# Turning the softmax maxima: a PE transpose in the first gap, or a float32r product in the gap of the first values

## Chip, cores and metric

The kernel is one program for one core of a Trainium2 chip. The metric is device time in microseconds (us) of one execution on that core, taken as the median of several runs. The engines that matter here are PE (TensorE, the matrix engine; the profile lists its weight loads apart, as PEld), ACT (ScalarE), DVE (VectorE), POOL (GpSimd) and SP, which here only issues DMAs.

## What is computed

The reference is one transformer block on 32 sequences of 512 tokens and 256 channels. Attention has 16 heads of 16 channels and two passes; the second pass attends over the error that the first one leaves. A small mixture of experts follows, which only touches the first sequence, and two layer norms. Cut to what matters here:

```python
qk = x @ W_attn + b_attn                      # q and k, 16 heads of 16
y  = softmax(mask(q @ k.T / sqrt(16))) @ v    # v = x by heads
e  = v[1:] - y[:-1]
k2 = x[:-1] @ W_k2 + b_k2
y2 = softmax(mask(q[1:] @ k2.T / sqrt(16))) @ e
x  = layernorm(x + proj(y) + proj(y2))
x  = layernorm(x + experts(x))                # experts: first sequence only
```

A softmax over keys needs the largest score of each query row. In the kernel these largest scores are the "maxima".

## The kernel before

**Groups and steps.** Four heads of one sequence are a group, so there are 32 x 4 = 128 groups. The function `step(n)` runs 132 times and works on several groups at once, as a pipeline: it finds the maxima of group n, computes the exponentials of group n-1 (first pass) and n-2 (second pass), and multiplies the exponentials of group n-2 with the values.

**Slots and gaps.** A step has five slots. A slot (`slot(n, s)`) is a stretch of small PE products that use 32 rows of the array each: score products for the maxima, which go to the PSUM tiles `sm` (L297, and their causal masks, L282), and score products for the exponentials, which go to the PSUM tiles `sc` (L361). The four heads are handled as two pairs. `slot` writes the order of these products out by hand: pair 1's exponentials and pair 0's maxima come first, then pair 0's exponentials and pair 1's maxima. Behind the maxima's products DVE finds the largest score of each row (L321, into `top`); behind the exponentials' products ACT takes the exponential (L378, `sc` to `pt`), four instructions in a slot.

After each slot comes a gap: products that use the whole array. The list `rest[s]` holds what is called in gap s. Gap 0 holds `augment(n-1)` in every step. In odd steps, half of a projection follows it (`project`, tile `pj`, L219, read out by ACT at L231 into `pk`). In even steps it is a quarter of an output projection (`attended`, tile `po`, L522, read out by DVE at L525 into `h`). Gap 1 holds the first values, `values(n-2, 0)` (tile `av`, L430), gaps 2 and 3 hold transposes of the attended values (`yt`, L445) and more of the projections, and gap 4 the second values. Eight steps, from n = 12 on, hold a part of one expert in front of this (`gu`, L603, and others).

**The maxima's way.** DVE splits each maximum into two halves that float32r holds exactly, a rounded one and the rest (`halve`, L327 and L328, called at the end of gap 4), in the tile `mx`. `augment` in the next step turns `mx` with four 128x128 PE transposes into one PSUM bank, the tile `mt` (L334), and ACT copies it to SBUF as `m` (L336). The score products take `m` as a third term, `k == 2`, with a matrix of minus ones as the stationary operand, so that what comes out is score minus maximum. The products of slots 0 and 1 use the `m` of group n-2. Slot 2 is the first one that uses the `m` of group n-1: its third product of each stream.

**PSUM.** There are eight banks. Four of them are two pairs for `sm` (`pair_of_banks`, two buffers). The other four (`bank`, four buffers) are taken in rotation by everything else, in the order in which the products are written: four `sc` tiles in each slot, and one for each full-array tile in a gap. A product may write to its bank only after the tile that had it before has been read out.

```python
def bank(name):
    return psum.tile([P, T], F32, tag="one", name=name, bufs=4)
```

**Who sets the order.** PE's and SP's order is the order of the code (`manual_schedule`). On ACT, DVE and POOL a planner sets the order. A tile framework puts in all waits. `half(ap)` is a view of float32 data as float32r.

Of the kernel before, what the change touches and what calls it, by code (L numbers as in the profile page):

```python
# [9 lines left out]
F32 = mybir.dt.float32  # L10
# [7 lines left out]
P = 128  # L18
# [16 lines left out]
def half(ap):  # L35
    return ap.bitcast(F32R)
# [3 lines left out]
def block_kernel(  # L40
# [16 lines left out]
    nc = tc.nc  # L57
# [10 lines left out]
    const = ctx.enter_context(tc.tile_pool(name="const", bufs=1))  # L68
# [10 lines left out]
    def bank(name):  # L79
        return psum.tile([P, T], F32, tag="one", name=name, bufs=4)  # L80
# [60 lines left out]

    ident = const.tile([P, P], F32, name="ident")
    make_identity(nc, ident)
    mhalf = const.tile([P, NB], F32, name="mhalf")
    nc.gpsimd.memset(mhalf, -0.5)

# [31 lines left out]
    mx = [const.tile([P, NB, GH, HS], F32, name=f"mx{i}") for i in range(2)]  # L178
# [12 lines left out]
    def load(b):  # L191
        if b:
            load_turned(b)
        s = seqs[b]
        s["x"] = seq.tile([P, NB, C], F32, tag="x", name=f"x{b}")
        nc.sync.dma_start(s["x"], x[b].rearrange("(n p) c -> p n c", p=P))

    def load_next(b):

        s = seqs[b]  # L200
        s["xs"] = seq.tile([P, NB, C], F32, tag="xs", name=f"xs{b}")
        nc.sync.dma_start(s["xs"][:, 0 : NB - 1], x[b, 1 : T - P + 1].rearrange("(n p) c -> p n c", p=P))
        nc.sync.dma_start(s["xs"][0 : P - 1, NB - 1], x[b, T - P + 1 : T])
        nc.sync.dma_start(s["xs"][P - 1 : P, NB - 1], x[b, T - 1 : T])

    def prepare(n):
        b, g = divmod(n, NG)
        s = seqs[b]
        heads = slice(g * GH, (g + 1) * GH)
        nc.gpsimd.tensor_copy(  # L210
            by_head(v_pad)[:, :, heads, 0:HD], s["x"].rearrange("p n (h d) -> p n h d", d=HD)[:, :, heads]
        )
# [26 lines left out]
    def spread(two, m, which=range(2)):  # L239

        for k in which:
            n = 2 * two + k
            d = groups.setdefault(n, {})
            d["q"] = q_t[n % len(q_t)]
            d["kk"] = kk_t[n % len(kk_t)]
            rows = slice(k * GH * HD, (k + 1) * GH * HD)
            for i, t in enumerate(moving[two, m]):
                if m == 0:
                    for r in range(2):
                        nc.sync.dma_start(d["q"][r::2, i], t[rows])  # L250
                else:
                    nc.sync.dma_start(d["kk"][i::2, m - 1], t[rows])
        if 1 in which:
            del moving[two, m]
# [70 lines left out]
    def halve(n):  # L325
        t, top = mx[n % 2], groups[n]["top"]
        nc.vector.tensor_copy(half(t[:, :, :, 0:2]), top)  # L327
        nc.vector.tensor_sub(half(t[:, :, :, 2:4]), top, t[:, :, :, 0:2])  # L328

    def augment(n):  # L330
        d = groups[n]
        ps = bank(f"mt{n}")
        for i in range(NB):
            nc.tensor.transpose(ps[:, i * P : (i + 1) * P], mx[n % 2][:, i].rearrange("p h s -> p (h s)"), ident)  # L334
        d["m"] = grp.tile([P, T], F32, tag="m", name=f"m{n}")
        nc.scalar.copy(half(d["m"]), ps)  # L336

# [102 lines left out]
    def normalize(n, a):  # L440
        b, g = divmod(n, NG)
        d, s = groups[n], seqs[b]
        ps = bank(f"yt{n}_{a}")
        for i in range(NB):
            nc.tensor.transpose(ps[:, i * P : (i + 1) * P], d["avs", a][:, i * P : (i + 1) * P], ident)  # L445
        got = ps.rearrange("p (n h s) -> p n h s", h=GH, s=HS)
        if a:

            kept = work.tile([P, NB, GH, HV], F32, tag="kept", name=f"kept{n}", bufs=2)
            nc.scalar.copy(kept, got[:, :, :, 0:HV])  # L450
            got = kept
        rden = small.tile([P, NB, GH], F32, tag="rden", name=f"rden{n}_{a}")
        sums = got[:, :, :, HD]
        if a:

            den = small.tile([P, NB, GH], F32, tag="den", name=f"den{n}")
            nc.vector.tensor_scalar_max(den, sums, 1e-30)
            sums = den
        nc.vector.reciprocal(rden, sums)
        rb = rden.unsqueeze(3).to_broadcast([P, NB, GH, HD])  # L460
        cols = slice(g * GH * HD, (g + 1) * GH * HD)

        def heads(t):
            return t[:, :, cols].rearrange("p n (h d) -> p n h d", d=HD)

        if a == 0:
            if g == 0:
                s["y"] = seq.tile([P, NB, C], F32, tag="y", name=f"y{b}")
            nc.vector.tensor_mul(heads(s["y"]), got[:, :, :, 0:HD], rb)
            nc.gpsimd.tensor_sub(by_head(e_pad)[:, :, g * GH : (g + 1) * GH, 0:HD], heads(s["xs"]), heads(s["y"]))  # L470
        else:
            y2 = work.tile([P, NB, GH * HD], F32, tag="y2", name=f"y2_{n}", bufs=1)
            nc.vector.tensor_mul(y2.rearrange("p n (h d) -> p n h d", d=HD), got[:, :, :, 0:HD], rb)
            nc.gpsimd.tensor_add(s["y"][:, :, cols], s["y"][:, :, cols], y2)  # L474
            groups.pop(n)
# [174 lines left out]
    def step(n):  # L650
        ready = lambda k: 0 <= k < n_all
        rest = [[] for _ in units]
        b, r = divmod(n, NG)
        if r == 1 and b + 1 < B:
            load(b + 1)
        if r == 3 and b + 1 < B:
            load_next(b + 1)
        if ready(n):
            prepare(n)
        if ready(n - 3):  # L660
            rest[3].append(lambda: normalize(n - 3, 1))
        if ready(n):
            rest[4].append(lambda: halve(n))
        if ready(n - 1):
            rest[0].append(lambda: augment(n - 1))
        if ready(n - 2):
            soon = n > n_all
            rest[0 if soon else 1].append(lambda: values(n - 2, 0))
            rest[1 if soon else 2].append(lambda: normalize(n - 2, 0))
            rest[4].append(lambda: values(n - 2, 1))  # L670
        two = n // 2 + 1
        if ready(2 * two):
            if n % 2 == 0:
                rest[2].append(lambda: project(two, 1))
                rest[4].append(lambda: spread(two, 1))
            else:
                rest[2] += [lambda: project(two, 0), lambda: spread(two, 0)]
                rest[0].append(lambda: project(two, 2, 0, T // 2))
                rest[3] += [lambda: project(two, 2, T // 2), lambda: spread(two, 2)]
        b, r = divmod(n - 3, NG)  # L680
        if r == NG - 1 and 0 <= b < B:
            rest[4].append(lambda b=b: turn(b))

        for b in range(B):
            end = (b + 1) * NG - 1
            last = b == B - 1
            for part in range(2):
                if n == (end + 4 if last else min(end + 5 + 2 * part, n_all)):
                    for i in range(2 * part, 2 * part + 2):
                        rest[0 if last or i % 2 == 0 else 3].append(lambda b=b, i=i: attended(b, i))  # L690
                if n == (end + 3 if last else end + 4):
                    rest[1 + 2 * part].append(lambda b=b, part=part: biased(b, part))
            if n == (end + 2 if last else end + 3):
                rest[3].append(lambda b=b: load_residual(b))
            if 0 < b < B - 1 and n == end + 8:
                rest[1].append(lambda b=b: store(b))


        e = n - first_expert
        if e == -1:  # L700
            rest[4] += [route, turn_tokens, lambda: load_hidden(0), lambda: load_down(0)]
        if e == 0:
            rest[0].insert(0, biases)
        if 0 <= e < E:
            rest[3].insert(0, lambda: hidden(e, 0, 0))
            rest[4].insert(0, lambda: hidden(e, 0, 1))
        if 0 <= e - 1 < E:
            rest[0].insert(0, lambda: hidden(e - 1, 1, 0))
            rest[1].insert(0, lambda: hidden(e - 1, 1, 1))
            rest[2].insert(0, lambda: down(e - 1))  # L710
            if e < E:
                rest[1].append(lambda: load_hidden(e))
                rest[2].append(lambda: load_down(e))
        if e == E:
            rest[4].append(lambda: second_norm(0, moe["acc"]))
        for s in range(len(units)):
            slot(n, s)
            for f in rest[s]:
                f()
# [94 lines left out]
```

## Time and profile before

| what | value |
|---|---|
| median of 3 runs | 2659.15 us (2658.19 to 2659.2) |
| the profiled execution | 2655.88 us |
| its span, first to last instruction | 2654.2 us |
| mean granted TensorE clock | 0.990 of full speed |
| POOL busy | 1730.8 us, 65% of the span |
| transposes of the maxima, L334 | 512, in 128 sets of four |
| copies to `m`, L336 | 128, 78.7 us of ACT in all |

A line of the timeline has a start (us from the start of the trace), a length (us, from the first start to the last end of what is merged), engine, line, operation, the tile written and the tiles read, shapes and a count; in brackets the engine's idle time before it and what ended that. The matmuls' ends are modelled, and matmuls overlap, so on PE the starts tell more than the lengths. In a weight load or matmul such as `mt<-ident,mx` the moving operand stands first and the stationary one second. The chain of work follows the last instruction back through what released each step.

### The profile page before, as it was taken

To read this page: it belongs to the slowest core of one execution; us is meant where nothing else is said; L and a number is where in the kernel's file an instruction comes from. 1 tells how busy PE (TensorE), PEld (TensorE's weight loads), DVE (VectorE), ACT (ScalarE), POOL (GpSimd) and SP (SyncE) were. 2 spreads that over 40 slices of the span, in tenths; PEclk is the share of its full clock that TensorE was granted. 3 is DMA by queue.
4 is the path that set the end of the run, shared out by engine and by line. 5 is a ranking of instruction groups with operands and counts; after the bars stand their busy time and mean duration, and the time that the engine had idled before them with its cause. 6 is when DMAs were issued, how large, how long until landed. Compare 5 with 4: busy or idle time off the path is not lost.

```text
span 2654.2 us, 98011 instructions
## 1 busy us (share of the span) xinstructions
PE 2593.7 (98%) x41488; PEld 1800.0 (68%) x41488; DVE 1936.3 (73%) x3225; ACT 1757.9 (66%) x3416; POOL 1730.8 (65%) x3303
## 2 busy tenths in 40 slices
PE   7999999999999999999999999999999999999997
PEld 4666666667676666666677667666776767677765
DVE  6767777677777777777777777777777777777773
ACT  3766544467667766766776677676777667677774
POOL 4555555466666667666666666666766666676664
PEclk8999999999999999999999999999999999999998
DMA  5323233233333333333333333342333334333320
GB/s 142 88 75 85 73 89 95 70 85 102 81 92 87 93 94 82 102 84 83 96 86 101 82 97 89 75 105 82 99 88 93 93 75 104 82 90 96 88 67 25
DMA packets 167461, 233.26 MB, mean 88 GB/s; under 512 B 21528, under 2 KB 91152, under 8 KB 167024
## 3 DMA queue, kind: packets, MB, share of 16 engines
q1 hardware_dynamic: 164592, 226.54, 32.9%
q8 instruction: 329, 5.39, 0.9%
q14 instruction: 108, 0.88, 0.1%
q10 hardware_dynamic: 2368, 0.42, 0.1%
q0 software_dynamic: 64, 0.02, 0.0%
HBM read 75.41 MB, written 16.78 MB: 35 GB/s over the span
## 4 chain that ended last, share of the span: by engine, by line
PE 90%; ACT 5%; issue 2%; DVE 2%; POOL 1%; DMA 0%; ACTq 0%; POOLq 0%; SPq 0%; DVEq 0%
PE av L430 22%; PE sc L361 20%; PE pj L219 13%; PE sm L297 10%; PE sm L282 7%; PE yt L445 6%; ACT pt L378 5%; PE po L522 4%; PE mt L334 3%; PE gu L603 2%; PE ys L511 1%; PE dn L626 1%; DVE top L321 1%; POOL xr L503 0%; POOL h L544 0%
## 5 line engine op out<-in xcount | busy, mean ns | idle before, releaser
L321 DVE TENSOR_REDUCE top<-sm 128x2 f32<-128x768 f32 (+3 forms) x1800 | 1536.4, 907 | 611.2 <-PE sm L297 610.6
L378 ACT ACTIVATE pt<-sc 128x512 f32<-128x512 f32 (+1 forms) x2564 | 1323.8, 601 | 333.8 <-PE sc L361 198.0
L382 POOL TENSOR_SCALAR_AFFINE_SELECT pt<-pt 128x256 f32<-128x256 f32 x2048 | 789.9, 410 | 520.2 <-ACT pt L378 519.8
L297 PE MATMUL sm<-kk_t,q_t 32*128 32x512 f32 (+2 forms) x7168 | 1100.0, 382 | 16.7 <-DVE top L321 9.3
L361 PE MATMUL sc<-q_t,kk_t 32*128 32x256 f32 (+3 forms) x8192 | 1028.2, 334 | 3.0 <-DVE h L525 1.8
L361 PEld LDWEIGHTS sc<-q_t,kk_t 32*128 32x128 f32 x8192 | 678.5, 184 | 257.5 <-issue 160.2
L361 PE MATMUL sc<-m,minus 32*128 32x256 f32 (+3 forms) x4096 | 694.6, 318 | 0.0
L297 PEld LDWEIGHTS sm<-kk_t,q_t 32*128 32x128 f32 x7168 | 567.6, 185 | 23.1 <-DVE top L321 12.2
L282 PE MATMUL sm<-hide,pick 32*128 32x64 bf16 (+5 forms) x10240 | 517.7, 217 | 0.0
L361 PEld LDWEIGHTS sc<-m,minus 32*128 32x128 f32 x4096 | 441.2, 185 | 10.0
L219 PE MATMUL pj<-xT,wq_sb 128*128 128x256 f32 (+1 forms) x1020 | 397.7, 513 | 6.3 <-DVE wq_sb L112 6.3
L438 ACT COPY avs<-av 128x512 f32<-128x512 f32 x256 | 150.4, 588 | 324.7 <-PE av L430 324.7
L430 PE MATMUL av<-pt,e_pad 128*32 128x512 f32 (+3 forms) x4096 | 304.3, 437 | 7.5 <-ACT pt L378 0.8
L430 PE MATMUL av<-pt,v_pad 128*32 128x512 f32 (+3 forms) x4096 | 302.7, 435 | 8.3 <-POOL pt L382 5.0
L231 ACT ACTIVATE pk<-pj,bp_qk 128x256 f32<-128x256 f32 (+1 forms) x255 | 151.3, 593 | 190.3 <-PE pj L219 182.7
L237 POOL TENSOR_TENSOR pk<-pk,lead 128x512 fp32r<-128x512 f32 x192 | 244.9, 1276 | 14.3 <-ACT lead L236 3.6
L430 PEld LDWEIGHTS av<-pt,v_pad 128*32 128x32 f32 x4096 | 136.3, 109 | 163.0 <-issue 126.9
L282 PEld LDWEIGHTS <-pick 32*128 32x128 bf16 x10240 | 243.7, 93 | 0.9 <-issue 0.7
L219 PEld LDWEIGHTS pj<-xT,wq_sb 128*128 128x128 f32 x1020 | 175.5, 192 | 92.1 <-issue 64.3
L430 PEld LDWEIGHTS av<-pt,e_pad 128*32 128x32 f32 x4096 | 128.9, 110 | 144.0 <-issue 135.6
L474 POOL TENSOR_TENSOR y<-y,y 128x256 f32<-128x256 f32 x128 | 96.6, 755 | 125.4 <-DVE mv L538 58.0
L445 PE MATMUL yt<-ident,avs 128*128 128x128 f32 x1024 | 168.0, 287 | 6.0 <-ACT pt L378 1.0
(90 smaller groups left out, 1955.1 us busy)
## 6 DMA issues: line engine op xcount, KB each, us to landing
q_t<-lead SPq DMA_DIRECT2D x256, 128.0 KB
q_t<-pk SPq DMA_DIRECT2D x256, 128.0 KB
kk_t<-lead SPq DMA_DIRECT2D x256, 128.0 KB
kk_t<-pk SPq DMA_DIRECT2D x256, 128.0 KB
xT<-in_xT SPq DMA_DIRECT2D x32, 512.0 KB
x<-in_x SPq DMA_DIRECT2D x32, 512.0 KB
xr<-in_x SPq DMA_DIRECT2D x32, 512.0 KB
out<-h SPq DMA_DIRECT2D x31, 512.0 KB
```

Source lines behind the costliest of these rows:

```text
L219: nc.tensor.matmul(ps[:, 0 : hi - lo], wq_sb[:, m, c, part * P : (part + 1) * P], seqs[b]["xT"][:, c, lo:hi], start=(c == 0), stop=(c == N ...
L231: nc.scalar.activation(pk[:, lo:hi], ps[:, 0 : hi - lo], AF.Identity, bias=bp_qk[:, m, part : part + 1])
L237: nc.gpsimd.tensor_sub(half(pk), pk, lead)
L282: nc.tensor.matmul(ps[hh][:, 0 if alone else hh].rearrange("p (k c) -> p k c", c=P)[:, first::step, HS * c :], pick[rows, c], hide[rows, c ...
L297: nc.tensor.matmul(part(ps[hh], i, na, at)[:, 0 if alone else hh], half(d["q"][rows, k, i * P : (i + 1) * P]), half(d["kk"][rows, a : a + ...
L321: nc.vector.tensor_reduce(to, view, AX.X, ALU.max)
L361: nc.tensor.matmul(ps[hh][:, at * P : at * P + T - j * P], half(keys), half(queries[:, j * P :]), start=(k == 0), stop=(k == 2),)
L378: nc.scalar.activation(pt[:, hh, lo:hi], ps[hh][:, lo:hi], AF.Exp, scale=HD**-0.5)
L382: nc.gpsimd.affine_select(diag, diag, pattern=[[0, NH2], [1, P]], compare_op=ALU.is_ge, fill=0.0, base=-a, channel_multiplier=-1,)
L430: nc.tensor.matmul(ps[HS * h : HS * (h + 1), j * P :], vals[:, j, (g * GH + h) * HV : (g * GH + h) * HV + HS], d["pt", a, j, h // NH2][:, ...
L438: nc.scalar.copy(avs, ps)
L445: nc.tensor.transpose(ps[:, i * P : (i + 1) * P], d["avs", a][:, i * P : (i + 1) * P], ident)
```

## The change

The four transposes become four ordinary products in float32r. The stationary operand is the same block of `mx`, now read as float32r, and the moving operand is an identity that is read as float32r too; a copy of the identity is rounded for it once at the start. The call moves from `rest[0]` to `rest[1]`, where it stands in front of `values(n-2, 0)`. The ACT copy to `m` is the same and moves along.

```diff
     ident = const.tile([P, P], F32, name="ident")
     make_identity(nc, ident)
+    ident_half = const.tile([P, P], F32, name="ident_half")
+    nc.vector.tensor_copy(half(ident_half), ident)
...
     def augment(n):
         d = groups[n]
         ps = bank(f"mt{n}")
         for i in range(NB):
-            nc.tensor.transpose(ps[:, i * P : (i + 1) * P], mx[n % 2][:, i].rearrange("p h s -> p (h s)"), ident)
+            nc.tensor.matmul(
+                ps[:, i * P : (i + 1) * P],
+                half(mx[n % 2][:, i].rearrange("p h s -> p (h s)")),
+                half(ident_half),
+                start=True,
+                stop=True,
+            )
         d["m"] = grp.tile([P, T], F32, tag="m", name=f"m{n}")
         nc.scalar.copy(half(d["m"]), ps)
...
         if ready(n - 1):
-            rest[0].append(lambda: augment(n - 1))
+            rest[1].append(lambda: augment(n - 1))
         if ready(n - 2):
             soon = n > n_all
             rest[0 if soon else 1].append(lambda: values(n - 2, 0))
```

## Prediction

> **What bounds the kernel.** I read the page's busy rows and its chain first, then the waits of PE's weight loads, then the timeline of two neighbouring steps, engine by engine.
>
> ```profile
> PE 2593.7 (98%) x41488; PEld 1800.0 (68%) x41488; DVE 1936.3 (73%) x3225; ACT 1757.9 (66%) x3416; POOL 1730.8 (65%) x3303
> PE 90%; ACT 5%; issue 2%; DVE 2%; POOL 1%; DMA 0%; ACTq 0%; POOLq 0%; SPq 0%; DVEq 0%
> PEld mt L334 <- ACT pt L378: 25.5, 124, 0.5
> PEld sc L361 <- DVE h L525: 2.8, 5, 0.7
> ```
>
> PE's own work sets the time: 98% busy, 90% of the chain. DVE, ACT and POOL each idle for a quarter of the span or more, but they hand out the PSUM banks, so they can still hold PE at a certain product. Work that only moves from one gap to another should cost PE nothing; the question is which bank is not free when PE comes earlier. That needs the timeline. First an even step (output projection in gap 0): PE's rows, the load of one later product, DVE's rows and ACT's rows.
>
> ```profile
> 1320.95 0.66 PE L334 MATMUL mt<-ident,mx 128*128 128x128 f32 x4
> 1321.44 1.12 PE L522 MATMUL po<-wp_sb,ysT 128*128 128x256 f32 x4
> 1322.49 0.45 PE L361 MATMUL sc<-q_t,kk_t 32*128 32x384 f32 x2
> 1323.31 0.18 PEld L361 LDWEIGHTS sc<-q_t,kk_t 32*128 32x128 f32 x2
> 1324.40 1.07 PE L430 MATMUL av<-pt,v_pad 128*32 128x512 f32 x8
> ...
> 1320.45 2.48 DVE L321 TENSOR_REDUCE top<-sm 128x2 f32<-128x768 f32 x4 [1.08 <-PE sm L297]
> 1322.85 0.41 DVE L525 TENSOR_TENSOR h<-po,xr 128x256 f32<-128x256 f32 x1
> ...
> 1320.29 2.06 ACT L378 ACTIVATE pt<-sc 128x512 f32<-128x512 f32 x4 [0.28 <-PE sm L297]
> 1322.22 0.62 ACT L336 CAST m<-mt 128x512 fp32r<-128x512 f32 x1
> ```
>
> The turning takes PE from 1320.95 to 1321.44, 0.49 us. Slot 1 runs from 1322.49 to 1324.40, where the first values start. The load at 1323.31 is the one to watch: it is the first product of slot 1 that writes the last of its four banks, and in the rotation that bank is the one `po` had. It comes 0.05 us after the `h` addition has ended (1322.85 + 0.41 = 1323.26). So already now PE meets that addition almost to the point. The addition itself waits for no PE work any more; it stands behind slot 0's four reductions on DVE, which run without a break from 1320.45 to 1322.93.
>
> An odd step has half a projection in place of `po`; rows of ACT, DVE and the loads:
>
> ```profile
> 1303.05 0.62 ACT L336 CAST m<-mt 128x512 fp32r<-128x512 f32 x1
> 1303.51 0.52 ACT L231 ACTIVATE pk<-pj,bp_qk 128x256 f32<-128x256 f32 x1
> ...
> 1301.28 2.48 DVE L321 TENSOR_REDUCE top<-sm 128x2 f32<-128x768 f32 x4 [1.18 <-PE sm L297]
> ...
> 1303.32 0.18 PEld L361 LDWEIGHTS sc<-q_t,kk_t 32*128 32x128 f32 x2 [0.33 <-ACT pt L378]
> 1304.09 0.21 PEld L361 LDWEIGHTS sc<-q_t,kk_t 32*128 32x128 f32 x2
> 1304.17 0.20 PEld L297 LDWEIGHTS sm<-kk_t,q_t 32*128 32x128 f32 x2
> ```
>
> Here the same product (1304.09) follows the copy to `pk`, which ended at 1304.03 behind the copy to `m`.
>
> **The change, part by part.** *Out of gap 0: 0.49 us a step.* The mean wait of the first load for an exponential's bank, 25.5 us over 124 sets or 0.2 us, lies under products still in flight. `po` or `pj` takes the place and the bank of `mt`, and slot 1 could start 0.49 us earlier. Its first two banks are now those of the second and third exponential of slot 0 (before, third and fourth): the four run 0.5 us apart, the third ends near 1321.85, and slot 1 would start at 1322.00. No wait there.
>
> *Even steps: the gain meets DVE.* The last bank is still the one of `po`. Slot 0 has not moved, so the reductions still end at 1322.93 and the addition at 1323.26. Left alone, the product would load 0.77 us after the slot's start (the distance in the odd step, 1304.09 - 1303.32), at 1322.77. It must wait until 1323.31, and PE's queue is in order, so everything behind it waits too: the rest of slot 1 and gap 1. The 0.49 us are all lost, and slot 1 ends at 1324.40 as before. Then the turning, now in gap 1, comes on top.
>
> *Odd steps: the gain is kept.* ACT no longer has `m` between the exponentials and `pk`, so `pk` ends near 1303.6, and the product that needs its bank would load at 1303.32 - 0.49 + 0.77 = 1303.60: no wait worth counting. Next late is the product that loads at 1304.17, pair 1's first maxima product: it would come at 1303.68, but its `sm` banks are free only when slot 0's reductions end, 1301.28 + 2.48 = 1303.76. That is a wait of about 0.1 us, about what the present hold behind `pk` costs. The turning comes back in gap 1, so the step nets 0, within -0.05 and +0.1.
>
> *Into gap 1: 0.44 us a step.* In the steps with an expert product at the head of gap 0 the exponentials' banks come free earlier; there `mt` starts at 372.69 and `po` at 373.13 (timeline of PE). Those 0.44 us, 0.11 us for each transpose, I take as the width where nothing waits. For the new form no row exists. From below: in the groups by form `sc<-q_t,kk_t` takes 431 ns with 512 columns and 369 with 384, so 128 float32r columns stream in some 0.06 us; if only the streams counted, four would take 0.25 us. From above: loads of 183 ns (`sc<-m,minus`) that overlap with nothing, plus the streams, 0.97 us. The nearest rows are two float32r products of 128 columns, one behind the other on the same rows of the array:
>
> ```profile
> 1323.95 0.18 PEld L361 LDWEIGHTS sc<-q_t,kk_t 32*128 32x128 f32 x1
> 1324.06 0.19 PEld L361 LDWEIGHTS sc<-m,minus 32*128 32x128 f32 x1
> ```
>
> They follow each other by 0.11 us, the pitch of the transposes. These use 32 rows and the new ones 128. I take 0.44 us.
>
> A rule speaks against the swap: the Trainium skill, "Perfetto Trace Analysis", section "Transposes", says to turn data with the transpose and not with an ordinary matmul, because the transpose skips the arithmetic. "TensorE: Matmul & The Clock Gate", section "Terms", gives the mode as four times faster for FP32. Taken literally, four products would take 1.76 us and the change +1.3 us in 123 steps, +160 us more. The 0.11 us pitch of float32r above speaks against that; the rule's factor is for plain FP32. I weigh it as a rival.
>
> *What covers the rest.* In gap 1 the turning needs the bank of slot 1's first exponential and the values that of the second; the present values already take the first one, so no new wait. The copy to `m` moves behind slot 1's exponentials on ACT. In the even step they end near 1325.4 and `m` near 1326.0, while slot 2 starts no earlier than the end of the values (2.36 us long in the chain), near 1327.2: over 1 us of cover. `mx` is ready earlier still. No DMA is issued by `augment`; SP and POOL hold nothing of it and it passes nothing of theirs that waits for it. The rounded identity is one DVE copy at the start, about 0.2 us as the casts to `minus` (228 ns), while PE still waits for weights: nothing.
>
> *Sum.* `po` follows `mt` in 60 even steps and `pj` in 63 odd ones (from the code's conditions; the other 5 of the 128 count as nothing). 60 x 0.44 us = 26 us; 63 x 0 = 0. Against the profiled execution: 2655.88 (span 2654.2 and 1.7 around it) + 26 = 2682. The median of the runs lies 3.3 us above that execution, so 2685 us, +1.0%. About 0.2% (5 us) is what a measurement here can tell from no change.
>
> **Rivals.**
> *Faster, 2647 us.* If the planner put the `h` addition in front of pair 1's reductions, or the rotation gave its bank later, both kinds of step keep the earlier slot 1 and also lose the present holds. Slot 1 takes 1.91 us now (1322.49 to 1324.40), but 1.75 us in the expert step (374.09 to 375.84). With some 0.1 us saved in 123 steps: -12 us. It decides if the addition ends within 0.77 us of slot 1's start. Against it: the addition stands behind the reductions in the code as on DVE now, and their input is ready earlier.
> *No change, 2659 us.* The turning is only moved: even steps keep part of the gain, since the bank rotation or the order differs from my reading, and odd steps are neutral. For it: PE is the bound and its work is the same.
> *Far slower, 2715 us.* The loads for 128 rows don't overlap with the streams, as the rule suggests. At 0.25 us more per set (four loads at 0.183 us in place of 0.11, less the shorter last stream of 0.06 in place of 0.11), 123 sets cost 31 us on top.
> *ACT's order, 2790 us.* If the copy to `m` went behind the copy of the values (L438, 0.59 us) it would end 1.2 us after slot 2's start, while its first reader loads about 0.3 us after it: 0.85 us in 123 steps, 105 us on top. Against it: its input is ready over 2 us earlier.
>
> **Numbers.** My forecast 0.66, with 2677 to 2701 as its own range (0.35 to 0.6 us in even steps, -0.05 to +0.1 in odd ones); faster 0.12; no change 0.09; far slower 0.10; ACT's order 0.03. Slower by over 0.2% is then 0.79. For 8 in 10 I leave out the faster case and ACT's order, 0.15 together: 2656 to 2715.
>
> **What would show it.** Right: in even steps the product of slot 1 loads just behind the `h` addition, about 1.3 us after the slot's start, and the row of `sc` loads waiting for `h` grows from 2.8 us to some 30 us; in odd steps `sm` loads wait a little for `top`; the matmuls of `mt` still follow each other by 0.11 us, with loads of 183 ns in place of 140. Wrong: `h` on DVE ahead of pair 1's reductions, a pitch of `mt` near 0.2 us, or `sc` products of slot 2 that wait for `m`.

## The result, and the profile after

| | before | after |
|---|---|---|
| median | 2659.18 us (4 runs) | 2698.97 us (4 runs, 2698.35 to 2700.79) |
| span of the profiled execution | 2654.2 us | 2697.5 us |
| mean granted TensorE clock | 0.990 | 0.991 |

The ratio is 1.0164, with a 95% interval from 1.0150 to 1.0177: slower by about 40 us. The forecast was 2685 us, +26 us. The sign and the mechanism were right; the size was short by 14 us, mainly in one term, the width of the turning in its new place.

Line numbers are shifted in the changed kernel: L299 stands for the maxima's products, L221 for `pj`, L323 for the reductions, L337 for the turning, L345 for the copy to `m`, L370 for the `sc` products, L387 for the exponentials, L439 for the values, L531 for `po` and L534 for the `h` addition. In the kernels of the experiments they can be a few lines off again. First the page of the changed kernel, busy rows and chain:

```profile
PE 2629.6 (97%) x41488; PEld 1802.7 (67%) x41488; DVE 1935.5 (72%) x3226; ACT 1764.1 (65%) x3416; POOL 1730.3 (64%) x3303
PE 84%; DVE 6%; ACT 5%; issue 2%; POOL 2%; DMA 0%; ACTq 0%; POOLq 0%; DVEq 0%
```

PE's number of instructions is the same, and DVE has its one cast more. But the chain runs through DVE for 6% of the span, where it was 2%. The list of waits says at which product (waits of the weight loads, then of the matmuls):

```profile
PEld sc L370 <- DVE h L534: 23.4, 60, 0.7
...
PE sc L370 <- DVE h L534: 11.7, 59, 0.5
```

Sixty waits, one for each even step with an output projection in gap 0, 23.4 us in all; before there were five of them, 2.8 us in all. The timeline of such an even step, PE and one weight load, then DVE:

```profile
947.90 1.13 PE L531 MATMUL po<-wp_sb,ysT 128*128 128x256 f32 x4
948.96 0.44 PE L370 MATMUL sc<-q_t,kk_t 32*128 32x384 f32 x2
950.27 0.18 PEld L370 LDWEIGHTS sc<-q_t,kk_t 32*128 32x128 f32 x2 [0.38 <-DVE h L534]
951.27 0.66 PE L337 MATMUL mt<-ident_half,mx 128*128 128x128 f32 x4
951.86 1.07 PE L439 MATMUL av<-pt,v_pad 128*32 128x512 f32 x8
...
947.40 2.48 DVE L323 TENSOR_REDUCE top<-sm 128x2 f32<-128x768 f32 x4 [1.08 <-PE sm L299]
949.80 0.41 DVE L534 TENSOR_TENSOR h<-po,xr 128x256 f32<-128x256 f32 x1
```

Slot 1 starts at 948.96. The product that needs `po`'s bank loads at 950.27, 1.31 us later, 0.06 us after the `h` addition ends (950.21). Slot 1 takes 2.31 us to the turning. The turning itself takes 0.59 us, from 951.27 to 951.86. An odd step:

```profile
928.58 1.13 PE L221 MATMUL pj<-xT,wq_sb 128*128 128x256 f32 x4
929.64 0.44 PE L370 MATMUL sc<-q_t,kk_t 32*128 32x384 f32 x2
931.59 0.66 PE L337 MATMUL mt<-ident_half,mx 128*128 128x128 f32 x4
932.18 0.64 PE L439 MATMUL av<-pt,v_pad 128*32 128x512 f32 x4
...
928.08 2.48 DVE L323 TENSOR_REDUCE top<-sm 128x2 f32<-128x768 f32 x4 [1.01 <-PE sm L299]
930.68 0.21 PEld L299 LDWEIGHTS sm<-kk_t,q_t 32*128 32x128 f32 x2
```

Here slot 1 takes 1.95 us. Pair 1's first maxima product loads at 930.68, 1.04 us after the start of the slot, 0.12 us after slot 0's four reductions end (928.08 + 2.48 = 930.56); before it loaded after 0.85 us. The list of waits doesn't count this one, since other loads fill the time (`sm` loads waiting for `top`: 7 waits, 12.2 us, in both kernels). The turning again takes 0.59 us.

I averaged the two traces by steps, from the first matmul of each stretch to that of the next. Where ordinary steps are counted below, these are 109 of the 132:

| us in a step | even, 55 steps | odd, 27 steps | odd after a `turn`, 27 steps |
|---|---|---|---|
| gap 0, from 1.54 to 1.06 | -0.48 | -0.48 | -0.48 |
| slot 1 | 1.91 to 2.31, +0.40 | 1.91 to 1.94, +0.03 | 1.82 to 1.95, +0.13 |
| turning in gap 1 | +0.59 | +0.59 | +0.59 |
| the whole step | +0.51 | +0.14 | +0.24 |

55 x 0.51 + 27 x 0.14 + 27 x 0.24 = 38 us of the 43 by which the two profiled spans differ; the rest lies in the steps that are not counted, with an expert's work or at the ends of the pipeline. Slots 2 to 4 and their gaps are the same to 0.01 us.

### The profile page after: what moved, and what is told of

It is laid out like the page before. It is cut to its first block, busy times and chain, and to the rows that moved or that the text cites. A ratio compares the mean times of both kernels' runs of the same rounds, so it can differ in the third digit from the quotient of the medians.

```text
span 2697.5 us, 97968 instructions
## 1 busy us (share of the span) xinstructions
PE 2629.6 (97%) x41488; PEld 1802.7 (67%) x41488; DVE 1935.5 (72%) x3226; ACT 1764.1 (65%) x3416; POOL 1730.3 (64%) x3303
## 4 chain that ended last, share of the span: by engine, by line
PE 84%; DVE 6%; ACT 5%; issue 2%; POOL 2%; DMA 0%; ACTq 0%; POOLq 0%; DVEq 0%
PE av L439 21%; PE sc L370 18%; PE pj L221 13%; PE sm L299 9%; PE sm L284 6%; PE yt L454 6%; DVE top L323 5%; ACT pt L387 5%; PE mt L337 3%; PE po L531 3%; PE gu L612 2%; PE ys L520 1%; PE dn L635 1%; DVE h L534 1%; POOL pk L239 0%
## 5 line engine op out<-in xcount | busy, mean ns | idle before, releaser
L323 DVE TENSOR_REDUCE top<-sm 128x2 f32<-128x768 f32 (+3 forms) x1800 | 1536.5, 907 | 660.1 <-PE sm L299 655.6
L387 ACT ACTIVATE pt<-sc 128x512 f32<-128x512 f32 (+1 forms) x2564 | 1330.0, 601 | 336.7 <-PE sc L370 194.9
L299 PE MATMUL sm<-kk_t,q_t 32*128 32x512 f32 (+2 forms) x7168 | 1112.7, 383 | 18.0 <-DVE top L323 10.3
L370 PE MATMUL sc<-q_t,kk_t 32*128 32x256 f32 (+3 forms) x8192 | 1047.1, 335 | 12.2 <-DVE h L534 11.7
L370 PEld LDWEIGHTS sc<-q_t,kk_t 32*128 32x128 f32 x8192 | 678.9, 184 | 278.3 <-issue 163.5
L370 PE MATMUL sc<-m,minus 32*128 32x256 f32 (+3 forms) x4096 | 697.8, 318 | 0.0
L299 PEld LDWEIGHTS sm<-kk_t,q_t 32*128 32x128 f32 x7168 | 567.8, 185 | 26.0 <-DVE top L323 12.2
L370 PEld LDWEIGHTS sc<-m,minus 32*128 32x128 f32 x4096 | 440.1, 184 | 9.9
L221 PE MATMUL pj<-xT,wq_sb 128*128 128x256 f32 (+1 forms) x1020 | 400.0, 516 | 6.7 <-DVE wq_sb L112 6.3
L439 PE MATMUL av<-pt,e_pad 128*32 128x512 f32 (+3 forms) x4096 | 303.8, 437 | 7.6 <-ACT pt L387 0.8
L439 PE MATMUL av<-pt,v_pad 128*32 128x512 f32 (+3 forms) x4096 | 305.0, 438 | 4.7 <-POOL pt L391 4.7
L221 PEld LDWEIGHTS pj<-xT,wq_sb 128*128 128x128 f32 x1020 | 175.9, 192 | 103.6 <-issue 66.4
L439 PEld LDWEIGHTS av<-pt,v_pad 128*32 128x32 f32 x4096 | 120.3, 110 | 164.3 <-issue 114.9
L439 PEld LDWEIGHTS av<-pt,e_pad 128*32 128x32 f32 x4096 | 127.7, 110 | 144.9 <-issue 136.0
```

The source lines that it names most:

```text
L221: nc.tensor.matmul(ps[:, 0 : hi - lo], wq_sb[:, m, c, part * P : (part + 1) * P], seqs[b]["xT"][:, c, lo:hi], start=(c == 0), stop=(c == N ...
L299: nc.tensor.matmul(part(ps[hh], i, na, at)[:, 0 if alone else hh], half(d["q"][rows, k, i * P : (i + 1) * P]), half(d["kk"][rows, a : a + ...
L323: nc.vector.tensor_reduce(to, view, AX.X, ALU.max)
L370: nc.tensor.matmul(ps[hh][:, at * P : at * P + T - j * P], half(keys), half(queries[:, j * P :]), start=(k == 0), stop=(k == 2),)
L387: nc.scalar.activation(pt[:, hh, lo:hi], ps[hh][:, lo:hi], AF.Exp, scale=HD**-0.5)
L439: nc.tensor.matmul(ps[HS * h : HS * (h + 1), j * P :], vals[:, j, (g * GH + h) * HV : (g * GH + h) * HV + HS], d["pt", a, j, h // NH2][:, ...
```

## Experiments

**Is it the place or the product?** `move_alone` keeps the transposes and moves the call; `swap_alone` takes the product and leaves the call.

```diff
# move_alone, on the kernel before
-            rest[0].append(lambda: augment(n - 1))
+            rest[1].append(lambda: augment(n - 1))
# swap_alone, on the changed kernel
-            rest[1].append(lambda: augment(n - 1))
+            rest[0].append(lambda: augment(n - 1))
```

> The four transposes stay transposes; only the call moves from gap 0 to gap 1. Theory (place): the whole cost comes from the place. In even steps slot 1 still waits for the h addition (+0.40 us), and the turning costs 0.59 us in front of the values and not 0.49[...]. Then this kernel takes about what the changed one does: 2695 to 2702 us. Rival (product): the float32r product itself is dearer than the transpose by 0.1 to 0.15 us a set; then the move alone is that much cheaper in 123 steps: 2680 to 2687 us.

> The product takes the place of the transposes, the call stays in gap 0. Theory (place): the product costs what the transposes cost, 0.11 us each: 2655 to 2663 us, no change that can be measured. Rival (product): 0.1 to 0.15 us more in each of 123 steps: 2671 to 2678 us.

The move alone takes 2699.56 us, ratio 1.0150 (1.0135 to 1.0165): all of the loss. The swap alone takes 2664.06 us, 1.0016 (1.0009 to 1.0023). The rows of `mt`, of `move_alone` first and then of `swap_alone` (count, then shortest, median and longest in ns):

```profile
L334 PEld LDWEIGHTS mt<-ident,mx x512: 138/140/146, 44.9 to 2651.3; 128*128 128x128 f32 x171
L334 PE MATMUL mt<-ident,mx x512: 272/273/336, 44.9 to 2651.4; 128*128 128x128 f32 x171
...
L337 PEld LDWEIGHTS mt<-ident_half,mx x512: 186/192/333, 42.0 to 2613.2; 128*128 128x128 f32 x171
L337 PE MATMUL mt<-ident_half,mx x512: 272/275/624, 42.0 to 2613.3; 128*128 128x128 f32 x171
```

The product's loads are 52 ns longer, and that shows nowhere: the matmuls follow each other by 0.11 us in both forms (the spacing of the starts, median). In gap 0 a set takes 0.50 us as products and 0.49 as transposes; in gap 1 it takes 0.59 us in both forms. So the whole loss comes from the place; the form makes 0.01 us a set.

The swap alone came out 5 us above the kernel before, a little over its range. About 4 us of that lie in the nine steps with an expert's work, where the planner put ACT and DVE in another order. ACT and DVE of `swap_alone` in one of these:

```profile
382.28 0.63 ACT L624 ACTIVATE sig<-hf 128x512 f32<-128x512 f32 x1 [1.53 <-DVE hf L620]
382.82 0.57 ACT L345 CAST m<-mt 128x512 fp32r<-128x512 f32 x1
...
382.95 0.69 DVE L625 SCALAR_TENSOR_TENSOR sig<-sig,hf 128x512 f32<-128x512 f32 x1 [0.70 <-ACT sig L624]
383.56 0.42 DVE L534 TENSOR_TENSOR h<-po,xr 128x256 f32<-128x256 f32 x1
```

The copy to `m` stands behind the expert's `sig` here and the `h` addition behind DVE's work on it. In the kernel before, `m` (373.33) went ahead of `sig` (373.81) and `h` (374.19) ahead of that work (374.54). Slot 1 takes 2.40 us in this step and took 1.75. These instructions take as long as before, within 0.02 us; only their order is another. In the changed kernel the `h` addition goes ahead of the expert's work again (at 380.05 and 380.86 in this step), and slot 1 of the steps with an expert's work takes 1.93 us on average, against 2.21 in `swap_alone` and 1.82 before.

**What does one set cost beyond its ends?** `turn_twice` issues each set twice.

```diff
-        for i in range(NB):
+        for i in [*range(NB), *range(NB)]:
             nc.tensor.matmul(
```

> The changed kernel with each set of four products issued twice into the same bank. Theory: the products follow each other by 0.11 us and the 0.15 us above 0.44 lie at the ends of the set, which are there once: 127 x 0.44 = +56 us on the changed kernel, 2755 us. Rival (each product costs 0.15 us): 127 x 0.59 = +75 us, 2774 us. If part of the second set hides in a wait that is there anyway: below 2750 us.

2756.71 us, 57.7 us above the changed kernel; each `mt` stretch takes 1.04 us in place of 0.59. A second set costs 0.45 us. So 0.44 was the right width of the four products, and 0.15 us come with the ends of a set in this place, once. The kernel before already had rows for that, which the prediction didn't use. In a few steps `mt` stands alone in gap 0, between two slots. PE's timeline of one of them:

```profile
93.84 0.66 PE L334 MATMUL mt<-ident,mx 128*128 128x128 f32 x4
94.43 0.43 PE L361 MATMUL sc<-q_t,kk_t 32*128 32x384 f32 x1
```

That is 0.59 us, with transposes, in gap 0. The other row is the turning `ys` in gap 4 (`turn`), also between products that use part of the array:

```profile
1338.41 1.09 PE L511 MATMUL ys<-ident,y 128*128 128x128 f32 x8
1339.43 0.49 PE L361 MATMUL sc<-q_t,kk_t 32*128 32x512 f32 x2
```

Eight transposes from 1338.41 to 1339.43 are 1.02 us, 8 x 0.11 + 0.14. The values in front of it take 2.29 us with `ys` and without.

The starts of the single products, as medians over a kernel's sets, split the 0.15 us in two:

| transposes of `mt` | first to second | last to what follows | the set |
|---|---|---|---|
| behind `gu`, before `po` or `pj` (before, expert steps) | 0.11 | 0.11 | 0.44 |
| behind a slot, before `po` or `pj` (before) | 0.165 | 0.11 | 0.49 |
| behind `gu`, before the values (`move_alone`, expert steps) | 0.11 | 0.20 | 0.53 |
| behind a slot, before the values (`move_alone`) | 0.165 | 0.20 | 0.59 |

So 0.055 us come where the set follows a slot, and gap 0 had that part too; 0.09 us come where the values follow it, and that part is new. The products of the changed kernel show the same two parts behind a slot (0.165 and 0.20). Why the second product behind a slot, and the values behind the set, start later no run here shows.

**Is it `po`'s bank?** `act_reads_po` changes only how the bank of gap 0's output projection is freed.

```diff
+        if b < B - 1 and i % 2 == 0:
+            got = work.tile([P, C], F32, tag="got", name=f"got{b}_{i}", bufs=1)
+            nc.scalar.copy(got, ps[:, 0:C])
+            nc.vector.tensor_add(s["h"][:, i], got, s["xr"][:, i])
+        else:
             nc.vector.tensor_add(s["h"][:, i], ps[:, 0:C], s["xr"][:, i])
```

> The changed kernel, but in even steps ACT copies the output projection of gap 0 out of its bank, and DVE adds from the copy. Theory (bank): slot 1 waits in even steps because po's bank is free only after the h addition behind slot 0's reductions; ACT has it out right behind slot 0's exponentials, so slot 1 keeps only the 0.03 to 0.13 us hold behind the reductions that odd steps have. Slot 1 in even steps from 2.31 to about 1.95 us, 60 x 0.36 = -22 us: 2674 to 2681 us. Rival (the reductions themselves hold slot 1, by the sm banks, and the bank of po only seems to): no change, 2697 to 2701 us.

2682.01 us, ratio to the kernel before 1.0089 (1.0074 to 1.0104), and 17 us under the changed kernel. Its even step, ACT, PE and DVE:

```profile
945.64 0.41 ACT L536 COPY got<-po 128x256 f32<-128x256 f32 x1
...
945.44 0.44 PE L370 MATMUL sc<-q_t,kk_t 32*128 32x384 f32 x2
947.38 0.66 PE L337 MATMUL mt<-ident_half,mx 128*128 128x128 f32 x4
...
946.28 0.41 DVE L537 TENSOR_TENSOR h<-got,xr 128x256 f32<-128x256 f32 x1
```

The bank is free at 946.05, 0.61 us after the start of slot 1, while the addition still ends only at 946.69. Slot 1 takes 1.95 us in place of 2.31, as the odd steps do. So the bank it was; the addition's own time does not matter. The total lies 1 us above the expected range: 60 x 0.36 = 22 us were expected, 17 measured. By steps, the 55 even ones became 0.34 us shorter (20.20 to 19.86 on average), which is 19 us. The ten steps around the expert's work became 0.27 us longer (28.63 to 28.89), which takes 3 us of that back.

**And what holds the odd steps?** `short_red_after` and, as its control, `short_red_before` let pair 1's reductions of slot 0 read only half of their keys.

```diff
             for view, to in views:
+                if u == 0 and pair == 1:
+                    view = view[..., 0 : view.shape[-1] // 2]
                 nc.vector.tensor_reduce(to, view, AX.X, ALU.max)
```

> The changed kernel with the second pair's reductions of slot 0 over half of their keys only (a part of the maxima is left out, so the numbers that come out differ). These reductions end about 0.5 us earlier, and the h addition behind them too. Theory (DVE's chain holds slot 1): in even steps the h addition ends before slot 1 needs its bank, slot 1 goes from 2.31 to about 1.85 us; in odd steps the sm banks come free in time, slot 1 from 1.94 to about 1.85. Together 60 x 0.46 + 63 x 0.09 = -33 us: 2663 to 2670 us. Rival (odd steps are held by the first exponential of slot 1, whose bank the turning takes, and not by the reductions): odd steps stay at 1.94, 2670 to 2675 us.

> The same shorter reductions in the kernel before the change, as a control. Theory: there the h addition holds slot 1 by under 0.1 us and in even steps only, so at most 60 x 0.08 = 5 us can come of it: 2653 to 2659 us, and the gap between the two kernels shrinks from 40 to about 10 us. If the reductions were a bound of their own, this kernel would gain as much as the changed one, 30 us.

The changed kernel falls to 2663.47 us, 1.0028 (1.0020 to 1.0036) of the kernel before; the control stays at 2656.93, 0.9997 (0.9989 to 1.0006). DVE and PE of the changed kernel with short reductions, even step:

```profile
975.75 1.95 DVE L325 TENSOR_REDUCE top<-sm 128x2 f32<-128x768 f32 x4 [1.08 <-PE sm L299]
977.62 0.42 DVE L536 TENSOR_TENSOR h<-po,xr 128x256 f32<-128x256 f32 x1
...
977.32 0.44 PE L372 MATMUL sc<-q_t,kk_t 32*128 32x384 f32 x2
979.13 0.66 PE L339 MATMUL mt<-ident_half,mx 128*128 128x128 f32 x4
979.72 1.07 PE L441 MATMUL av<-pt,v_pad 128*32 128x512 f32 x8
```

The addition ends at 978.04, 0.72 us after slot 1's start, and slot 1 takes 1.81 us; the median is 1.82 in even and odd steps alike. In odd steps pair 1's first maxima product loads 0.85 us after the start of slot 1 again. So the odd steps were held by the reductions and not by slot 1's first exponential, although the list of the changed kernel puts 62 waits of the turning down to it (14.9 us). In the odd step shown above that exponential ends at 931.41, 0.18 us before the turning loads at 931.59; here the turning loads at 979.13, 0.05 us behind it.

Half a microsecond of DVE work in front of slot 1 is worth 35 us in the changed kernel and nothing before. The same DVE work, the same reductions: only the place of four PE products decides whether PE meets it. The turning still takes 0.59 us, and the two kernels with short reductions differ by 6.5 us. That is what the move costs without the hold behind the reductions: 0.59 - 0.48 = 0.11 us in a step, most of it given back where slot 1 falls from 1.91 to 1.82.

The control also corrects a reading. In it the product that needs `po`'s bank no longer waits for the addition, yet slot 1 takes 1.91 us as before. Its ACT and PE rows show why:

```profile
974.31 1.57 ACT L380 ACTIVATE pt<-sc 128x512 f32<-128x512 f32 x3 [0.83 <-PE sc L363]
...
973.13 0.44 PE L363 MATMUL sc<-q_t,kk_t 32*128 32x384 f32 x2
975.05 1.07 PE L432 MATMUL av<-pt,v_pad 128*32 128x512 f32 x8
```

The first exponential of slot 1 starts at 974.31 and takes about 0.6 us; the values take its bank and start at 975.05. So before the change the values waited for that exponential, and the small hold behind the addition was hidden under it.

**Does the freed bank help the kernel before?** `act_reads_po_before` makes the edit of `act_reads_po` there.

> The kernel before the change, with the output projection of gap 0 copied out by ACT in even steps. This could beat it if the hold of under 0.1 us behind the h addition goes. But ACT comes to that copy only behind the copy to m, at about the time at which the h addition ends now: 2655 to 2660 us, no change expected. If the exponentials are pushed back by the extra copy: up to 60 x 0.4 = +24 us.

2654.24 us, 0.9986 (0.9979 to 0.9993). This is the fastest kernel of the study, by 0.14%: the interval leaves out 1, but the gain is below the 0.2% that the forecast took as what can be told here. On average its even steps take 19.71 us against 19.69 before and its odd ones 0.02 to 0.04 us less than before, so the trace shows no place where the 3 us come from.

## Why the prediction was right, point by point

- *PE sets the time, and moved work costs what it meets.* Right: slots 2 to 4 did not change.
- *Even steps: the gain of gap 0 meets DVE.* Right, with the wait at the product named, 1.31 us after the start of the slot as forecast, and shown by `act_reads_po` and `short_red_after`. The list of waits has 23.4 us for it, where some 30 were forecast. The loss in slot 1 was 0.40 us and not the whole 0.49, since slot 1 before was held to 1.91 us by its first exponential, which the longer slot 1 now covers.
- *Odd steps: the net is 0.* Too good by 0.14 to 0.24 us, beyond the +0.1 that the forecast allowed. The hold behind the reductions came (0.03 and 0.13 us of slot 1); the rest is the next point.
- *The turning in gap 1 costs 0.44 us.* This is the term that was mis-sized: it measured 0.59. I took the width from expert steps, where `mt` stands between two products that use the whole array, and read the 0.05 us more of gap 0 as a wait for an exponential's bank. It is not a wait: in even steps of the changed kernel that bank is free half a microsecond before the turning (the exponential ends at 950.72, `mt` loads at 951.26), and the 0.055 us behind a slot are there all the same. The 0.09 us in front of the values were nowhere in the forecast. 123 x 0.15 = 18 us, more than the 14 us that were missing; the smaller loss in slot 1 (60 x 0.09 = 5 us) goes the other way.
- *Product against transpose.* Right: the pitch is 0.11 us. The rule of the Trainium skill ("Perfetto Trace Analysis", section "Transposes"), weighed and set aside in the forecast, finds no cost here: the form made 0.01 us a set.
- *The copy to `m` is covered in gap 1.* Right: no wait for it is in the list.
- *The rivals.* The planner kept the addition behind the reductions, so the faster case never arose. Loads without overlap are excluded by the pitch. The fear of ACT's order showed up elsewhere, as `swap_alone`'s 4 us in the expert steps.

## What to carry to other kernels

A stretch of PE work that seems only to be worth its own time can also be the time that another engine needs: look which bank the next products take, who empties it, and what stands in front of that on its queue. Read the slack of each of these before moving work away, and move it only from places where the slack is larger than the work. Price moved work from a row with the same neighbours on both sides, not only of the same shape; here four turnings cost 0.44 us among whole-array products and 0.59 between products that use a part of it.

## What the runs showed of the hardware

- A 128x128 float32r product with an identity and a PE transpose of the same float32 data follow each other at the same 0.11 us, although the loads take 192 and 140 ns.
- A set of whole-array products between products on parts of the array costs about 0.15 us beyond its pitch, in both forms (0.59 us for four, 1.04 for eight; 1.02 for the eight of `ys`). For the four, 0.055 us lie behind the first product and 0.09 in front of what follows.
